# Attention scores in runs of two slot blocks and two heads, packed over five PSUM banks, with the context matmuls in one group

## The chip, the cores and the metric

The kernel runs on one core of a Trainium2 chip. The metric is the device time of one execution in microseconds. Names used for the engines: PE is TensorE (its matmuls; PEld its weight loads), ACT is ScalarE, DVE is VectorE, POOL is GpSimd and SP is SyncE, whose queue issues most transfers. L701 means line 701 of the kernel before.

## The reference

Sixteen batches of a residual self-attention with a mask. Each batch has 1024 tokens of 512 features, and 8 heads of 64 features. Queries, keys and values are the same projection `q`.

```python
def _L0_cond_ref(x, mask, Wq, Wo):          # x: (16, 512, 1024), mask: (16, 1024) of 0 and 1
    xt = jnp.transpose(x, (0, 2, 1))
    q = xt @ Wq.T
    qh = q.reshape(B, T, NH, dk).transpose(0, 2, 1, 3)
    scores = scale * jnp.einsum('bhqd,bhkd->bhqk', qh, qh)
    cmask = mask[:, None, None, :]
    rmask = mask[:, None, :, None]
    logits = (scores * cmask + (1.0 - cmask) * NEG) * rmask
    attn = jax.nn.softmax(logits, axis=-1)
    ctx = jnp.einsum('bhqk,bhkd->bhqd', attn, qh)
    ctx = ctx.transpose(0, 2, 1, 3).reshape(B, T, D)
    out = ctx @ Wo.T
    return jnp.transpose(out, (0, 2, 1))
x = x + _L0_cond_ref(x, cond_2048, L0_cond_Wq, L0_cond_Wo)
```

## The kernel before

**What it works on.** About half of the tokens of a batch are active (mask 1). The kernel sorts the active tokens of each batch into "slots", gathers their rows with indirect transfers, and does the attention over the slots only; the tokens with mask 0 all get one mean row. The width A of a batch is the number of slots that are computed: 544 for batches 0 to 4, 528 for batches 5 to 13, 512 for the last two. A slot block is 128 slots, so a batch has four whole blocks and, where A is over 512, a tail of 32 or 16 slots.

**Precision.** `query` (L513) projects with pairs of fp16 numbers, and the result q is again split into a high half h and a low half l, both fp16 (`qsplit`, L529 to L531). Four transfers on SP (L540 and on) lay them out per pair of heads in a tile `xx` of 128 partitions and four planes. For the first head of the pair, plane 0 holds h on partitions 0 to 63 and l on 64 to 127, and plane 1 holds l and h. Planes 2 and 3 hold the same for the second head.

**Scores** (`scores`, L701). For a head and a block, four matmuls: two column halves of A/2, and for each half two matmuls over all 128 partitions. Plane [h; l] against plane [h; l] gives h.h + l.l; against plane [l; h] it gives h.l + l.h. They write a tile `pss` of two PSUM banks, and the pool `ps_s` has two such tiles. ACT takes the exponential of the tile (L705), with the sum of each row as a second output (the row "ACTIVATION_READ_ACCUMULATOR"), into a tile `p` (12 buffers, which the tail's exponentials share).

**Tail scores** (L676) are those of the 32 tail slots of four heads at once: sixteen matmuls with 32 weight columns each, into a `pss` tile. ACT (L680) takes their exponential, DVE splits it, and four SP transfers (L692, L693) bring it to a tile `pt`.

**Context** (`attend`). For a pair of heads, 16 fp32 products (32 matmul records) with 64 weight columns each (L726) accumulate attention times values, head 0 into partitions 0 to 63 and head 1 into 64 to 127 of a tile `pav` of two banks (pool `ps_av`). The tail's part (L730) is added with two or four full-width matmuls, and ACT copies the result to a tile `c` (L734).

**The rest of PE's work**, called fill here: transposes of the gathered rows (`xt`, L486), the query projection (L513), values (L569), the output projection (`project`, L817) and small transposes for the softmax's shift and sums (L628, L637, L764). All of these write a pool `ps_m` of two single banks. These banks are emptied by ACT (q at L516, v at L572, the high half of x at L444) or DVE (the residual sum at L822, the low half of x at L445). So the eight banks are 4 for scores, 2 for context and 2 for all the rest.

**Order.** The loop in `run` goes over batches b, and in each over 18 steps: for each p from 0 to 3 (a pair of heads, 2p and 2p+1) the four blocks i, and two steps for the tail scores, at places 2 and 13. A step emits the scores of head 2p, some fill, the scores of head 2p+1, and fill again. The fill is one list `m` for the batch, in which pieces have costs; it belongs to the next batch's projection (n = b+1) and the previous batch's output (o = b-1). `share` says how much of it each step gets. The context group of a pair is emitted at the second step (i = 1) of the next pair, and its tail part at the third. Each step issues one indirect transfer on POOL from a list (`issue`). A scheduler orders each engine's instructions by their places in the program and by when they are ready in its own model; `behind` pins an instruction behind another on its engine, and `high_priority(offset=HPO)` moves one forward. The order on each engine is then fixed.

## Time and profile before

| what | value |
|---|---|
| median of 3 runs | 1041.18 us (1039.56 to 1042.92) |
| the profiled execution | 1033.88 us |
| its span, first to last instruction | 1032.2 us |
| mean granted TensorE clock | 0.995 |
| PE busy in 480 to 512 us | 31.49 of 32.00 us |
| ACT busy in 480 to 512 us | 22.42 of 32.00 us |
| DVE busy in 480 to 512 us | 22.17 of 32.00 us |
| first and last start of L701 | 33.1 and 1007.8 us |

A group line of the profile has the line, the engine, the operation and its tiles (written <- read), the shape and the count; then the busy time in us and the mean length in ns of one; then the idle time of the engine just before these instructions and what ended it. A busy time counts overlapping instructions once. The length of a matmul includes its way through the array, and the next one starts long before it ends, so the distance between starts tells what one costs. A shape such as 128*64 says that the weights have 128 rows and 64 columns. A line of the waits has who waited for whom: us in total, times, the longest.

### The profile page before, as it was taken

The numbers are of one execution on the slowest core, as the hardware profiler recorded it, in microseconds if no ns is written. First come the engines' busy times: TensorE is split into PE (matmuls) and PEld (weight loads), VectorE is DVE, ScalarE is ACT, GpSimd is POOL, SyncE is SP. The second block draws the span as 40 slices with busy tenths as digits, with TensorE's granted clock in tenths as the row PEclk, the third lists the DMA queues.
The fourth block names the chain that finished last, engine by engine and source line by source line (L and its number), as shares of the span: only waits on it lengthen the run. The fifth ranks groups of instructions, "written<-read, shape, count | busy, mean of one in ns | idle before, by whom it ended". The sixth has DMA issues, their size and how long they took to land. (4 is left out here: it accounts for less than half of the span.)

```text
span 1032.2 us, 23511 instructions
## 1 busy us (share of the span) xinstructions
PE 988.2 (96%) x8455; PEld 685.0 (66%) x8455; DVE 725.1 (70%) x2410; ACT 659.5 (64%) x1702; POOL 300.8 (29%) x307
## 2 busy tenths in 40 slices
PE   7798999999999999999999999999999999999996
PEld 6576667666676766767666676767666666776563
DVE  6897668676775767877666787767777777666653
ACT  5876767557667666667667567756667667665550
POOL 3101013223311232233232333323232322325562
PEclk9999999999999999999999999999999999999999
DMA  6746546557554586575657565576565666556652
GB/s 199 231 139 183 136 134 161 183 161 206 165 142 128 150 239 172 151 209 148 190 157 227 172 169 168 163 203 185 163 210 138 192 184 184 151 142 191 185 183 95
DMA packets 78795, 177.73 MB, mean 172 GB/s; under 512 B 14688, under 2 KB 20576, under 8 KB 78672
## 3 DMA queue, kind: packets, MB, share of 16 engines
q1 hardware_dynamic: 57584, 108.40, 38.8%
q0 software_dynamic: 21088, 67.75, 20.9%
q8 instruction: 69, 1.13, 0.5%
q14 instruction: 54, 0.44, 0.1%
HBM read 91.49 MB, written 33.91 MB: 121 GB/s over the span
## 5 line engine op out<-in xcount | busy, mean ns | idle before, releaser
L705 ACT ACTIVATE p<-pss,nm 128x528 f32<-128x528 f32 (+2 forms) x512 | 359.5, 706 | 169.6 <-PE pss L701 160.0
L701 PE MATMUL pss<-xx 128*128 128x264 f16 (+2 forms) x2048 | 300.9, 276 | 6.1 <-ACT p L705 5.2
L726 PE MATMUL pav<-p,v 128*64 128x264 f32 (+2 forms) x2048 | 243.3, 390 | 0.0
L701 PEld LDWEIGHTS <-xx 128*128 128x128 f16 x2048 | 194.2, 99 | 62.4 <-issue 25.1
L726 PEld LDWEIGHTS pav<-p,v 128*64 128x64 f32 x2048 | 141.4, 137 | 85.7 <-issue 13.5
L901 POOL DMA_INDIRECT y_out<-xa,idx x68 | 73.5, 1081 | 285.4 <-PE pss L701 101.6
L513 PE MATMUL pm<-xh,wqh 128*128 128x264 f16 (+5 forms) x512 | 142.2, 278 | 4.1 <-DVE xa L822 3.4
L513 PE MATMUL pm<-xl,wqh 128*128 128x264 f16 (+5 forms) x512 | 141.6, 277 | 0.2 <-DVE xl L445 0.2
L513 PE MATMUL pm<-xh,wql 128*128 128x264 f16 (+5 forms) x512 | 141.7, 277 | 0.0
L395 POOL DMA_INDIRECT xa<-x_in,idx x68 | 68.6, 1009 | 201.7 <-PE pss L701 81.1
L513 PEld LDWEIGHTS <-wqh 128*128 128x128 f16 x1024 | 98.3, 99 | 24.0 <-issue 7.5
L705 ACT ACTIVATION_READ_ACCUMULATOR p<-pss,nm 128x1 f32 x512 | 103.9, 203 | 0.0
L901 POOL DMA_INDIRECT y_out<-xi,idx x60 | 72.6, 1211 | 97.0 <-PE pss L701 26.5
L817 PE MATMUL pm<-woh,ch 128*128 128x512 f16 x240 | 91.1, 379 | 0.0
L817 PE MATMUL pm<-woh,cl 128*128 128x512 f16 x240 | 90.9, 379 | 0.0
L817 PE MATMUL pm<-wol,ch 128*128 128x512 f16 x240 | 90.9, 379 | 0.0
L395 POOL DMA_INDIRECT xi<-x_in,idx x60 | 61.3, 1021 | 95.3 <-PE pss L701 31.9
L516 ACT ACTIVATE q<-pm 128x264 f32<-128x264 f32 (+5 forms) x128 | 50.2, 392 | 59.9 <-PE pm L513 59.3
L822 DVE SCALAR_TENSOR_TENSOR xa<-pm,xa 128x512 f32<-128x512 f32 x60 | 41.3, 689 | 56.4 <-PE pm L817 52.7
L817 PEld LDWEIGHTS <-ch 128*128 128x128 f16 x480 | 46.1, 98 | 44.8 <-issue 0.9
L799 DVE TENSOR_TENSOR c<-c,rb 128x528 f32<-128x528 f32 (+2 forms) x64 | 45.4, 710 | 43.0 <-DMA rb<-rd 21.3
L888 DVE TENSOR_TENSOR xi<-xi,ub 128x512 f32<-128x512 f32 (+1 forms) x60 | 40.8, 688 | 41.8 <-PE pss L701 41.2
(223 smaller groups left out, 1509.6 us busy)
## 6 DMA issues: line engine op xcount, KB each, us to landing
xx<-hl SPq DMA_DIRECT2D x224, 136.0 KB
xm<-x_nat_in SPq DMA_DIRECT2D x56, 512.0 KB
rb<-rd SPq DMA_DIRECT2D x72, 132.0 KB
rb<-rd SPq DMA_DIRECT2D x40, 136.0 KB
pt<-c SPq DMA_DIRECT2D x36, 132.0 KB
pt<-p SPq DMA_DIRECT2D x36, 132.0 KB
ub<-ud SPq DMA_DIRECT2D x16, 256.0 KB
xx<-hl SPq DMA_DIRECT2D x32, 128.0 KB
```

The lines of the kernel that those rows point to most:

```text
L395: dma = self.nc.gpsimd.indirect_dma_start(out=tile[:n], out_offset=None, in_=self.x, in_offset=bass.IndirectOffsetOnAxis(ap=idx, axis=0))
L513: self.beat = nc.tensor.matmul(pq, lhsT=w[:, c, e * P:(e + 1) * P], rhs=xx[:, c, cols], start=(k == 0), stop=(k == 3 * DC - 1)).ins
L516: nc.scalar.activation(s["q"][:, e, cols], pq, AF.Copy, scale=1.0 / (SX * SW))
L701: self.beat = nc.tensor.matmul(pt[:, g, :CH], lhsT=xx[:, 2 * k, i * P:(i + 1) * P], rhs=xx[:, 2 * k + a, g * CH:(g + 1) * CH], start=(a == ...
L705: self.exp = [nc.scalar.activation(t.rearrange("p (g c) -> p g c", g=2), pt[:, :, :CH], AF.Exp, bias=s["nm"][p // HG][:, p % HG:p % HG + 1 ...
L726: mm = nc.tensor.matmul(s["pav"][k * DK:(k + 1) * DK, g, :CH], lhsT=s["v"][p][:, i, k * DK:(k + 1) * DK], rhs=ps[k][:, cols], start=(i == ...
L799: self.once(nc.vector.tensor_tensor(c[:, :A], c[:, :A], s["rb"][p], ALU.mult), self.beat if p < 3 else None)
L817: nc.tensor.matmul(po[:cols.stop - cols.start], lhsT=a[:, e, cols], rhs=w[:, e, :], start=(e == 0 and k == 0), stop=(e == DC - 1 and k == 2))
L822: self.nc.vector.scalar_tensor_tensor(x, po, 1.0 / (SX * SW), x, ALU.mult, ALU.add)
L888: self.once(self.nc.vector.tensor_tensor(x[:n], x[:n], s["ub"][:n], ALU.add), self.beat)
L901: dma = self.nc.gpsimd.indirect_dma_start(out=self.out, out_offset=bass.IndirectOffsetOnAxis(ap=idx, axis=0), in_=x, in_offset=None)
```

## The change

**Scores.** `scores(b, p, u)` now does a pair of heads p and two slot blocks (2u and 2u+1) in one run of 16 matmuls, so there are eight runs a batch, at the steps i = 0 and i = 2. The four results ("places": head 0 and 1, block 0 and 1 of each) lie one behind the other, A columns each, in the first five banks of one tile of six banks, from column `FIRST[A]` on. A matmul can't cross a bank, so each place is cut where a bank ends. The cross terms h.l + l.h are done as before on 128 partitions. The product h.h is done with 64 partitions of weights: plane 0's partitions 0 to 63 for the first head, plane 3's partitions 64 to 127 for the second. The two heads' pieces are issued in turn and never share a bank; the one piece that would (the second place's end, from column 1024 on) stays on 128 partitions. The product l.l is left out, except in that piece. All matmuls of a run are pinned behind one another. The first waits for all exponentials of the run before (`left`), which ACT does in the order of places 3, 0, 1, 2.

**Context.** `attend` does a pair's whole context at once, right behind the first run of the next pair, in banks 4 and 5 of the same tile from column 240 on: first the half in bank 5, then the half in bank 4 (which the fourth place reaches too, so it waits for that exponential), then the tail's part and the copy. The next run's matmuls in bank 4 wait for the copy.

**Around it.** The tail scores use banks 0 and 1 of the tile and move to places 3 and 12 of the steps. The fill's shares change to almost nothing behind the first run and most of it behind the second. The copies of q and v on ACT get `high_priority`. The first step of each pair issues two indirect transfers on POOL. Some pieces of fill change places, and a piece of cost 1.0 that does nothing is put in.

```diff
+FIRST = {544: 40, 528: 54, 512: 0}
...
-        self.ps_s = pool("ps_s", 2, space=PS)
-        self.ps_av = pool("ps_av", 1, space=PS)
         self.ps_m = pool("ps_m", 2, space=PS)
+        self.begun = ExitStack()
+        self.ps_0 = self.begun.enter_context(tc.tile_pool(name="ps_0", bufs=2, space=PS))
+        self.ps_w = self.begun.enter_context(tc.tile_pool(name="ps_w", bufs=1, space=PS))
+        self.context_out, self.left = None, []
+        self.main = lambda: pool("ps_s", 1, space=PS).tile([P, 6, 512], F32, tag="s", name="pss")
...
+    def needs(self, i, *others):
+        for o in others:
+            self.tc.add_manual_dep(i, o.name, mybir.DependencyInfo(mybir.DependencyClass.Sync, mybir.DependencyReason.DATA),
+                                   reason="the same banks")
+
+    def other_banks(self, i, *others):
+        for o in others:
+            self.tc.declare_no_dep(i, o, reason="other banks")
...
-        nc.scalar.activation(s["q"][:, e, cols], pq, AF.Copy, scale=1.0 / (SX * SW))
+        with self.tc.high_priority(offset=HPO):
+            nc.scalar.activation(s["q"][:, e, cols], pq, AF.Copy, scale=1.0 / (SX * SW))
...
-        nc.scalar.copy(v, pv)
+        with self.tc.high_priority(offset=HPO):
+            nc.scalar.copy(v, pv)
...
-            pt = self.ps_s.tile([P, 2, 512], F32, tag="s", name="pss")
+            pt = self.ps[:, 0:2]
...
+    def scores(self, b, p, u):
...
+        xx = s["xx"][p]
+        flat = self.ps.rearrange("p k n -> p (k n)")
+        first = FIRST[A]
+        places = [(k, 2 * u + i, first + (2 * k + i) * A) for k in range(2) for i in range(2)]
+        last = []
+        out = self.context_out
+
+        calls, lanes = [], ([], [])
+        for j, (k, i, at) in enumerate(places):
+            rows = slice(i * P, (i + 1) * P)
+            h = xx[k * DK:(k + 1) * DK, 3 * k, :]
+            cuts = [at] + [c for c in (512 * (j + 1),) if at < c < at + A] + [at + A]
+            for c0, c1 in zip(cuts, cuts[1:]):
+                cols = slice(c0 - at, c1 - at)
+                calls.append((c0, c1, xx[:, 2 * k, rows], xx[:, 2 * k + 1, cols]))
+                if j == 1 and c0 == 1024:
+                    calls.append((c0, c1, xx[:, 2 * k, rows], xx[:, 2 * k, cols]))
+                else:
+                    lanes[k].append((c0, c1, h[:, rows], h[:, cols]))
+        for j in range(max(map(len, lanes))):
+            calls += [l[j] for l in lanes if j < len(l)]
+        banks = [c[0] // 512 for c in calls]
+        for n, (c0, c1, w, x) in enumerate(calls):
+            with self.behind(*last), self.tc.high_priority(offset=HPO if n else 0):
+                m = nc.tensor.matmul(flat[:, c0:c1], lhsT=w, rhs=x, start=banks[n] not in banks[:n], stop=banks[n] not in banks[n + 1:])
+            if out and banks[n] < 4:
+                self.other_banks(m.ins, out)
+            elif out and banks[n] not in banks[:n]:
+                self.needs(m.ins, out)
+            if n == 0 and self.left:
+                self.needs(m.ins, *self.left)
+            last = [m.ins]
...
+        for j in (3, 0, 1, 2):
+            k, i, at = places[j]
+            t = self.sb([P, C], F32, "p", 12)[:, :A]
+            e = nc.scalar.activation(t, flat[:, at:at + A], AF.Exp, bias=s["nm"][p // 2][:, p % 2 * 2 + k:p % 2 * 2 + k + 1],
+                                     scale=SCALE, accum_out=s["z"][:, 2 * p + k, i:i + 1]).ins
...
+    def attend(self, b, p, after=None):
...
+        pav = self.ps[:, 4:6, 240:240 + CH]
+        first = []
+        exps = self.left if after else []
+        for g in (1, 0):
+            cols = slice(g * CH, (g + 1) * CH)
+            for i in range(3, -1, -1):
+                for k in (1, 0):
+                    with self.behind(*(first or ([after] if after else []))), self.tc.high_priority(offset=HPO):
+                        mm = nc.tensor.matmul(pav[k * DK:(k + 1) * DK, g], lhsT=s["v"][p][:, i, k * DK:(k + 1) * DK],
+                                              rhs=ps[k, i][:, cols], start=(i == 3), stop=(i == 0 and A == 512))
+                    self.other_banks(mm.ins, *exps[1 - g:])
+                    if g == 0 and i == 3:
+                        self.needs(mm.ins, *exps[:1])
+                    first = first or [mm.ins]
...
-        S.insert(2, (0, None))
-        S.insert(13, (1, None))
+        S.insert(3, (0, None))
+        S.insert(12, (1, None))
...
-                share = [(1.2, 0) if i is None else ((1.0, 0.6), (0.1, 0.5), (0.9, 1.0), (0.9, 0.9))[i] for _, i in S]
+                share = [(0, 0) if i is None else ((0, 0.3), (0.4, 0.4), (1.3, 1.3), (1.2, 1.2))[i] for _, i in S]
...
-                            self.scores(b, p, None)
-                    else:
-                        ps = [self.scores(b, 2 * p, i)]
-                        if i == 2 and whole:
-                            whole.pop()()
+                            self.tail_scores(b, p)
+                    elif i % 2 == 0:
+                        self.scores(b, p, i // 2)
                     fill(share[st][0], st == N - 1)
-                    if i is not None:
-                        ps.append(self.scores(b, 2 * p + 1, i))
...
+                    if i == 0:
+                        for f in todo:
+                            f(self.beat)
+                        todo = []
+
+                    for _ in range(1 + (i == 0) if b < B - 2 else -(-len(self.urgent + self.spare) // (N - st))):
                         self.issue()
...
-                            free.setdefault(st + 3 + (p == 2), []).append(L(self.recip_rows, b, p))
+                            free.setdefault(st + 3, []).append(L(self.recip_rows, b, p))
```

## The prediction

> **What bounds the kernel now.** I read the busy times first, then the costliest groups, then PE's order of time in the middle of the span, then the waits, then ACT's order of time. From the page:
>
> ```profile
> PE 988.2 (96%) x8455; PEld 685.0 (66%) x8455; DVE 725.1 (70%) x2410; ACT 659.5 (64%) x1702; POOL 300.8 (29%) x307
> L705 ACT ACTIVATE p<-pss,nm 128x528 f32<-128x528 f32 (+2 forms) x512 | 359.5, 706 | 169.6 <-PE pss L701 160.0
> L701 PE MATMUL pss<-xx 128*128 128x264 f16 (+2 forms) x2048 | 300.9, 276 | 6.1 <-ACT p L705 5.2
> L726 PE MATMUL pav<-p,v 128*64 128x264 f32 (+2 forms) x2048 | 243.3, 390 | 0.0
> ```
>
> ACT idles because it waits for PE's scores (169.6 us before the exponentials); PE hardly ever waits for ACT (5.2 us). So the end is set by how densely PE streams. The mean of 276 ns is no price, since matmuls overlap; the price is the distance between starts, in the timeline of PE:
>
> ```profile
> 481.09 0.61 PE L701 MATMUL pss<-xx 128*128 128x264 f16 x4
> 481.63 0.41 PE L486 MATMUL pm<-ident,xt 16*128 16x16 f32 x4
> 481.98 0.29 PE L513 MATMUL pm<-xh,wqh 128*128 128x264 f16 x1
> ...
> 490.14 0.61 PE L701 MATMUL pss<-xx 128*128 128x264 f16 x4
> 490.59 0.17 PE L307 MATMUL pm<-eh,on 128*128 128x3 f16 x1
> 490.61 0.61 PE L701 MATMUL pss<-xx 128*128 128x264 f16 x4
> 491.15 3.78 PE L726 MATMUL pav<-p,v 128*64 128x264 f32 x32
> 494.87 0.62 PE L701 MATMUL pss<-xx 128*128 128x264 f16 x4
> ...
> 516.48 0.38 PE L817 MATMUL pm<-wol,ch 128*128 128x512 f16 x1
> 516.70 0.38 PE L817 MATMUL pm<-woh,cl 128*128 128x512 f16 x1
> 517.01 0.63 PE L676 MATMUL pss<-xx 128*32 128x264 f16 x16
> 517.57 0.33 PE L628 MATMUL pm<-ident,smcol 128*128 128x128 f32 x1
> ```
>
> Read from it: four 264-column matmuls take 0.45 us (490.14 to 490.59), 0.1125 each; a 512-column one 0.216 (twelve starts from 514.33 to 516.70 average 0.2155). So a column costs 0.417 ns and a matmul 2.4 ns on top. From the last score to the context group 0.54 passes in place of 0.45 (490.61 to 491.15): the change of array shape costs 0.09. The same stands at L817 to L676 (517.01 less 516.70 is 0.31, not 0.216), at the way back (0.46 of matmul in 0.56, below), and into the 16-row transposes (481.63 less 481.09 is 0.54). I take **0.095 us a switch**. The sixteen 32-column-wide matmuls of L676 last 0.56 with a switch, so 0.46, 0.029 each: a quarter of 0.1125, four side by side. Narrow tiles do run together here.
>
> ACT and the waits:
>
> ```profile
> 503.95 0.70 ACT L705 ACTIVATE p<-pss,nm 128x528 f32<-128x528 f32 x1 [1.00 <-PE pss L701]
> 504.64 0.69 ACT L705 ACTIVATE p<-pss,nm 128x528 f32<-128x528 f32 x1
> 505.32 1.05 ACT L425 ACTIVATE xm<-xm 128x1024 f32<-128x1024 f32 x1
> 506.27 0.19 ACT L425 ACTIVATION_READ_ACCUMULATOR xm<-xm 128x1 f32 x1
> ```
> ```profile
> PE pss L701 <- ACT p L705: 5.2, 11, 0.6
> PE pav L730 <- DMA pt<-p: 6.0, 7, 1.8
> ```
>
> An exponential takes 0.69 us of ACT from start to start, its sum included. The eleven waits of a score matmul for ACT are 0.47 us each.
>
> **The change, part by part.**
>
> 1. *Fewer columns.* A run does one pair of heads and two blocks of 128 slots. Before, that is 16 matmuls of half the width A: 16 x 0.1125 = 1.80 us for A=528. After: the cross terms on all 128 rows, 4 x 528 columns in 8 pieces (cut at bank ends): 2112 x 0.417 + 8 x 2.4 = 0.900. One 86-column piece of h.h stays on 128 rows: 0.038. The other seven are on 64 rows: pieces of 458, 70, 442 columns in the lower half, 426, 102, 410, 118 in the upper, issued in turn. In order and side by side, the upper half ends last: 0.193 (first piece below), then 102 and 410 columns above start behind it, then 118: 0.463. Sum 1.401, saving 0.399. For A=544 the same working gives 1.853 - (0.927 + 0.046 + 0.489) = 0.391, for A=512 1.747 - (0.864 + 0.432) = 0.451. Five batches are 544 wide, nine 528, two 512, with 8 runs each: 15.6 + 28.7 + 7.2 = **-51.6 us**. No 64-row pair is in the trace. Bounds: if the halves do not overlap, the seven pieces cost 0.862, not 0.463, and 0.399 of saving is 0; perfect balance (2026 columns halved, 0.43) would give 4 us more. The 32-wide quads are the nearest row, so I take overlap. The small pieces have a second bound: the 16-row transposes take (0.35 - 0.095)/4 = 0.064 each where a 16-column matmul should need 0.01; if 64-row matmuls have that floor, three pieces per run lose about 0.02 each, 8 us in all.
>
> The Trainium skill, "TensorE: Matmul & The Clock Gate" (Part 3, "Measured speedup vs the span model"), lists 3.07x for four row tiles, so about 77% of the ideal; the L676 row has 97% for column tiles. By the page the two lanes would take 0.60 in place of 0.463, 18 us less gain.
>
> 2. *More switches.* Before, each pair of heads has two: into the context group and out. After: 128 rows to 64 rows, then to the 64-wide context group directly, then back; and in the second run two more. Three more for 64 pairs: 192 x 0.095 = **+18.2 us**.
>
> 3. *One score buffer in place of two.* The scores fill up to five banks, held once. The first matmul of a run waits for all four exponentials of the run before; all later work queued on PE stands behind it. From the last matmul's start, ACT starts 0.32 later (the fourth of the matmuls that start at 508.00 begins at 508.34, ACT at 508.66), so four exponentials are done after 0.32 + 4 x 0.69 + 0.1 = 3.2 us. What hides this: a pair lasts (1007.8 - 33.1)/64 = 15.2 us; without scores 3.6, context 3.8, its tail 0.35 and tail scores 0.3 it has 7.2 us of projections, which the new shares divide 1.1 to 5.0: 1.3 us behind the first run, together with 4.2 of context, and 5.9 behind the second. First run: 5.5 against 3.2, free. Second: 5.9 against 3.2 plus ACT's other work in that stretch. That is (659.5 - 512 x 0.69)/64 = 4.8 us a pair; less the context copy 0.6 and one half-batch sum 1.25 it is 2.95, and 5.0/6.1 of it is 2.4. So 0.3 us of slack: closed, but narrowly. The tail scores are worse: they move one step later (third place to fourth) and sit in banks 0 and 1 behind only 2.6/6.1 of 7.2 = 3.1 us. They come 0.1 us late at best, and by 1.4 if ACT did one sum first. I take the 0.45 of the waits now seen, for 28 tail groups: **+12.6 us**. Bounds of the whole part: nothing (PE order fills the holes with other projections) to 64 x 1.05 (a sum of 1.25 in front, less some slack) plus 28 x 1.0, 95 us. I am near the low end because the nearest row, L701's present wait, is rare.
>
> 4. *Context in one group behind the run.* The same 32 matmuls. Its first half uses bank 5, which no score holds; the second half needs bank 4, so the exponential of the fourth block, done 1.0 us after the run, against 1.8 us of first half: free, unless a sum of 1.25 us is ahead on ACT (then 0.4). The tail transfer pt is issued one step later and needed at the group's end, some 7 us later; landing now ends 7 waits of 6.0 us in all: from -6 to +6, taken 0. The copy of the context must be done before the next run reaches bank 4, 0.9 us into it; 1.3 us of projections and this hide its 0.6.
>
> 5. *At nothing:* copies of q (0.39) and v (0.6) go ahead of exponentials on ACT, which is the 2.4 above; two transfers instead of one are issued on POOL per first step, whose 29% hides it; the reciprocal of the third pair comes one step earlier, with three transfers on SP, whose queue gets pt's four a step later. Twelve p buffers hold eight of a pair, four of the next run and, for a while, a tail. If the tail's transfers land late, the fourth exponential waits; 3 us of margin cover this.
>
> Sum: -51.6 + 18.2 + 12.6 = -20.8. The profiled execution lasts 1033.88 (span 1032.2), so 1013.1. It is 0.7% under the median of 1041.18; the forecast for the median is 1041.2 - 20.8 = **1020.4 us**.
>
> **Rivals.**
>
> - *ACT takes the place of PE in the second half of each pair.* Four exponentials come at once where before one came every 1.9 us, so the evacuations that PE's two other buffers need stand in the same queue. It decides from (51.6 - 18.2 - 12.6)/64 = 0.33 us of stall in each second run, on top. At 0.8 (between 0.33 and 1.05 and nearer the top, as each pair has a sum) it costs 51 us: 1041.2 - 20.8 + 51 = 1071. For it: 0.3 us of slack. Against: ACT is at 64%, and sums may run during the 1.4 us of a score run, when it has no exponential. 0.19.
> - *The stalls are spread and eat the gain:* PE's other buffers are freed late by 0.08 us on the mean over 252 evacuations by ACT (128 q, 64 v, 60 xh), 20 us: 1041. Scores in small pieces no longer fill in between. 0.09.
> - *The halves don't overlap*, or both wait for one another at bank ends: no saving, 1041.2 + 18.2 + 12.6 = 1072. Against: the quads of L676. 0.06.
> - *Weights of a half can't be loaded under its own matmul.* The 16-row transposes at 0.064 hint at it. A load of 0.098 (L701's own row) exposed for 3.5 matmuls a run is 0.34, 44 us: 1064. Against: 32-wide quads at full rate with the same loads. 0.05. The Trainium skill's page just named has it, in "The mechanism": loads overlap matmuls only where the row group differs. L701 on full rows contradicts it, with loads hidden at 0.1125 spacing.
>
> **How the numbers follow.** The forecast has 0.61; its own range is 1003 (no stall at all: 1008, and some now seen waits gone) to 1036. What this measurement can tell from no change is about 0.3%, 3 us. Faster: 0.61 and a little of the second rival, 0.62. Within 0.3%: 0.08. Slower: 0.19 + 0.06 + 0.05, 0.30. The range 1002 to 1068 leaves out the no-overlap case, the upper half of ACT's and a little of the forecast: 0.19.
>
> **What would show it.** Right: h.h matmuls of the two halves starting in pairs; score runs of about 1.4 us plus a switch; PE's waits for p summing to 10 to 20 us, at the tail scores; context still 3.6. Wrong: waits of the first score matmul for p in most runs (ACT), or starts of 64-row matmuls one behind the other. It fails most easily on the second half's 0.3 us.

## The result, and the profile after

The changed kernel takes **1107.8 us** (median of four, 1102.99 to 1115.91) against 1041.65 us (1039.56 to 1042.92): 1.0645 times the time, with a 95% interval of 1.0579 to 1.0711. It is 66 us slower; the forecast was 1020.4, 21 us faster. The profiled execution took 1108.16 us, with a span of 1106.3 us (74.1 more than before) and a mean granted clock of 0.948 (0.995 before). The kernel before was profiled in an execution of 1033.88 us, below its median, which is why the spans differ by more than the medians.

The page of the changed kernel first: the busy times, the slices of granted clock, and the groups that answer to those of the prediction (L740 scores, L754 exponential, L774 context).

```profile
PE 1000.5 (90%) x8327; PEld 611.4 (55%) x8327; DVE 745.1 (67%) x2410; ACT 658.9 (60%) x1702; POOL 300.5 (27%) x307
PEclk8898899999999999899999999999899989999698
L754 ACT ACTIVATE p<-pss,nm 128x528 f32<-128x528 f32 (+2 forms) x512 | 355.4, 703 | 169.5 <-PE pss L740 131.5
L774 PE MATMUL pss<-p,v 128*64 128x264 f32 (+2 forms) x2048 | 245.4, 392 | 3.4 <-ACT p L754 3.4
L740 PE MATMUL pss<-xx 128*128 128x86 f16 (+31 forms) x1920 | 220.3, 287 | 11.1 <-issue 5.2
```

The scores' busy time fell from 300.9 to 220.3 us, and PE as a whole is busier than before: 1000.5 for 988.2. More busy time for less work means that something else on PE takes longer per instruction; a PEclk digit under 9 says where to look. PE is idle for 106 us of the span, where it was 44.

One stretch of steady state, at the head of batch 7, shows all of it in the timeline of PE (columns: start, length, engine, line, what it writes and reads, count, and in brackets the idle time before it with what ended that).

```profile
501.31 0.40 PE L582 MATMUL pm<-two,xx 128*128 128x64 f16 x8
501.54 1.67 PE L740 MATMUL pss<-xx 128*128 128x458 f16 x16
503.14 3.78 PE L774 MATMUL pss<-p,v 128*64 128x264 f32 x32
506.86 0.44 PE L608 MATMUL pm<-ident,qt 128*128 128x128 f32 x2
507.05 0.49 PE L782 MATMUL pss<-pt,vt 128*128 128x264 f32 x2
507.38 0.60 PE L498 MATMUL pm<-ident,xa 128*128 128x128 f32 x4
508.92 0.66 PE L498 MATMUL pm<-ident,xa 128*128 128x128 f32 x4 [0.94 <-DVE tmp L611]
509.41 1.67 PE L740 MATMUL pss<-xx 128*128 128x458 f16 x16
511.01 0.66 PE L498 MATMUL pm<-ident,xa 128*128 128x128 f32 x4
513.40 0.63 PE L498 MATMUL pm<-ident,xa 128*128 128x128 f32 x4 [1.73 <-DMA xa<-x_in,idx]
514.93 0.47 PE L582 MATMUL pm<-two,xx 128*128 128x64 f16 x8 [0.91 <-DVE xl L457]
515.53 0.33 PE L816 MATMUL pm<-ident,rcol 128*128 128x128 f32 x1
516.23 0.41 PE L498 MATMUL pm<-ident,xt 16*128 16x16 f32 x4 [0.37 <-DVE rr L819]
...
517.08 0.43 PE L525 MATMUL pm<-xh,wqh 128*128 128x264 f16 x1
517.30 0.43 PE L525 MATMUL pm<-xl,wqh 128*128 128x264 f16 x1
```

Three things are to be seen. A score run lasts 1.60 us from start to start (501.54 to 503.14, 509.41 to 511.01), and the context is still one group with the length it had. Then, at the head of the batch, PE waits four times between 507.98 and 516.23, 3.95 us in all: each time for a buffer of the pool `ps_m`, or for the rows that are to go through one. And behind these waits, from 516.86 on, a projection matmul takes 0.22 us from start to start where 0.1125 is its price. A table by stretch of the same place shows why (columns: stretch, length, busy time of each engine with its instructions, granted clock, share of the DMA engines, GB/s):

```profile
509.00:513.00 4.00, 2.67 (x24) 1.63 (x24) 2.10 (x4) 2.10 (x6) 2.35 (x3) 1.00 0.92 258
513.00:516.50 3.50, 1.69 (x17) 1.17 (x17) 1.57 (x3) 3.50 (x9) 0.97 (x1) 1.00 0.34 97
517.00:520.00 3.00, 3.00 (x27) 1.69 (x25) 3.00 (x9) 2.02 (x5) 0.00 (x0) 0.50 0.09 23
520.00:523.00 3.00, 3.00 (x36) 2.04 (x29) 1.79 (x7) 1.19 (x3) 0.92 (x1) 0.97 0.92 287
```

PE is busy for 58% of 7.5 us, the granted clock then drops to 0.50, for some 3.4 us, and comes back. So these waits are paid twice: once as idle time, and again as half speed behind them. The heads of the other batches are alike, though not the same: in each of the batches 1 to 13 PE waits between 7 and 16 us from the batch's first score matmul, 0.2 to 2.7 us at a time and 3.1 us in all on the mean, and the clock drops at 12 to 15 us. The wait for gathered rows stands in six of them.

The largest waits of PE in the whole trace (columns: who waits for whom; us in total, times, longest), and below them what is listed for `xl` in the kernel before:

```profile
PE pm L582 <- DVE xl L457: 11.9, 10, 2.2
PE pm L498 <- DMA xa<-x_in,idx: 9.5, 6, 2.7
PE pm L328 <- ACT q L529: 7.6, 9, 0.9
```

```profile
PE pm L594 <- DVE xl L445: 0.2, 1, 0.2
PE pm L513 <- DVE xl L445: 0.2, 1, 0.2
PE pm L764 <- DVE xl L445: 0.2, 1, 0.2
```

The head of batch 7 in the kernel before has eight transposes in one go, twice, with scores or the context between, and no wait:

```profile
471.60 1.06 PE L701 MATMUL pss<-xx 128*128 128x264 f16 x8
472.50 1.04 PE L486 MATMUL pm<-ident,xa 128*128 128x128 f32 x8
473.38 0.61 PE L701 MATMUL pss<-xx 128*128 128x264 f16 x4
473.92 3.78 PE L726 MATMUL pav<-p,v 128*64 128x264 f32 x32
477.63 1.09 PE L486 MATMUL pm<-ident,xa 128*128 128x128 f32 x8
478.56 1.06 PE L701 MATMUL pss<-xx 128*128 128x264 f16 x8
```

**The account.** Three sums over the records of PE in both traces: *idle* is the sum of all gaps over 40 ns; *half clock* is the time in which the granted clock was 0.5; *lost* is what the matmuls started in that time took beyond their price at full clock (columns x 0.417 ns + 2.4). Idle went from 36.2 to 98.9 us (+62.7), half clock from 12.2 us in 3 stretches to 117.3 us in 20, lost from 3.5 to 48.4 (+44.9). The two steps on scores save 51.6 - 18.2 = 33.4 us. So 62.7 + 44.9 - 33.4 = 74.2 us, and the span grew by 74.1. That the two agree so closely is partly luck: the 33.4 is the forecast's own figure, and another count of *lost* (half of the time at half clock in which PE isn't idle) gives +42.4 in place of +44.9.

In the 13 batches from 1 to 13, where the pattern repeats, a batch has 4.3 us of idle time (1.2 before) and 5.0 us at half clock (0 before) and lasts 3.6 us longer. (A batch is counted from its first score matmul to that of the next.) The rest is at the ends: batch 0 +7.4, batch 14 -6.4, batch 15 +25. Some 10 us of the last are a stop at 1033 to 1043 us, in which a score run stands still with nothing shown that it waits for, ACT and DVE do next to nothing either, and from 1035.6 on the clock is at half for 17.1 us. Of the other profiles only that of s1_after512 has such a stop, in the same score run. It stays unexplained, and whether the executions that were not profiled had it isn't known.

### The profile page after: what moved, and what is told of

The parts are those of the page before. It is cut to its first block, busy times and chain, and to the rows that moved or that the text cites. A ratio compares the mean times of both kernels' runs of the same rounds, so it can differ in the third digit from the quotient of the medians.

```text
span 1106.3 us, 23204 instructions
## 1 busy us (share of the span) xinstructions
PE 1000.5 (90%) x8327; PEld 611.4 (55%) x8327; DVE 745.1 (67%) x2410; ACT 658.9 (60%) x1702; POOL 300.5 (27%) x307
## 3 DMA queue, kind: packets, MB, share of 16 engines
q8 instruction: 68, 1.11, 0.4%
## 4 chain that ended last, share of the span: by engine, by line
PE 75%; ACT 8%; DVE 8%; DMA 4%; issue 3%; another core or an unknown queue 1%; POOL 1%; SPq 1%; POOLq 0%; DVEq 0%; ACTq 0%
PE pss L774 18%; PE pm L525 15%; PE pss L740 15%; PE pm L869 15%; ACT p L754 5%; PE pm L498 2%; PE pss L782 2%; PE pss L687 2%; DVE xl L457 2%; DMA xa<-x_in,idx 1%; PE pm L816 1%; PE pss L869 1%; PE warm L366 1%; DMA pt<-p 1%
## 5 line engine op out<-in xcount | busy, mean ns | idle before, releaser
L754 ACT ACTIVATE p<-pss,nm 128x528 f32<-128x528 f32 (+2 forms) x512 | 355.4, 703 | 169.5 <-PE pss L740 131.5
L774 PE MATMUL pss<-p,v 128*64 128x264 f32 (+2 forms) x2048 | 245.4, 392 | 3.4 <-ACT p L754 3.4
L740 PE MATMUL pss<-xx 128*128 128x86 f16 (+31 forms) x1920 | 220.3, 287 | 11.1 <-issue 5.2
L774 PEld LDWEIGHTS pss<-p,v 128*64 128x64 f32 x2048 | 142.0, 138 | 92.7 <-issue 17.5
L953 POOL DMA_INDIRECT y_out<-xa,idx x68 | 72.8, 1071 | 414.9 <-DVE xa L874 116.8
L740 PEld LDWEIGHTS <-xx 128*128 128x128 f16 (+1 forms) x1920 | 109.0, 97 | 95.0 <-issue 38.6
L525 PE MATMUL pm<-xh,wqh 128*128 128x264 f16 (+5 forms) x512 | 151.6, 296 | 3.8 <-DVE rr L819 1.2
L525 PE MATMUL pm<-xl,wqh 128*128 128x264 f16 (+5 forms) x512 | 151.2, 295 | 0.0
L525 PE MATMUL pm<-xh,wql 128*128 128x264 f16 (+5 forms) x512 | 151.0, 295 | 0.0
L407 POOL DMA_INDIRECT xa<-x_in,idx x68 | 77.1, 1134 | 115.6 <-ACT xm L437 49.1
L754 ACT ACTIVATION_READ_ACCUMULATOR p<-pss,nm 128x1 f32 x512 | 104.5, 204 | 0.0
L786 ACT COPY c<-pss 128x528 f32<-128x528 f32 (+2 forms) x64 | 38.4, 599 | 82.2 <-PE pss L782 43.1
L457 DVE SCALAR_TENSOR_TENSOR xl<-pm,xh 128x512 f16<-128x512 f32 (+2 forms) x73 | 42.8, 608 | 44.5 <-ACT xh L456 27.2
L874 DVE SCALAR_TENSOR_TENSOR xa<-pm,xa 128x512 f32<-128x512 f32 x60 | 41.2, 687 | 45.4 <-PE pm L869 37.3
```

The source lines that it names most:

```text
L407: dma = self.nc.gpsimd.indirect_dma_start(out=tile[:n], out_offset=None, in_=self.x, in_offset=bass.IndirectOffsetOnAxis(ap=idx, axis=0))
L457: self.xs = nc.vector.scalar_tensor_tensor(self.xl[dst], src, SX, self.xh[dst], ALU.mult, ALU.subtract).ins
L525: self.beat = nc.tensor.matmul(pq, lhsT=w[:, c, e * P:(e + 1) * P], rhs=xx[:, c, cols], start=(k == 0), stop=(k == 3 * DC - 1)).ins
L740: m = nc.tensor.matmul(flat[:, c0:c1], lhsT=w, rhs=x, start=banks[n] not in banks[:n], stop=banks[n] not in banks[n + 1:])
L754: e = nc.scalar.activation(t, flat[:, at:at + A], AF.Exp, bias=s["nm"][p // 2][:, p % 2 * 2 + k:p % 2 * 2 + k + 1], scale=SCALE, accum_out ...
L774: mm = nc.tensor.matmul(pav[k * DK:(k + 1) * DK, g], lhsT=s["v"][p][:, i, k * DK:(k + 1) * DK], rhs=ps[k, i][:, cols], start=(i == 3), sto ...
```

## The experiments

All ratios are to the kernel before on the same chip, and the intervals are 95%. Idle, half clock and lost are the sums just defined, and the last two columns are lengths of batches, all in us and from the profiled execution of each kernel. The executions were not all on one chip (the kernel before takes 1033.8 us on the one of e1 to e5 and some 1042 on the others), so the same batch of 65 us can differ by some 0.5 us between them; the ratios are free of this.

| kernel | ratio, interval | idle | half clock | lost | batches 1 to 13, mean | batch 15 |
|---|---|---|---|---|---|---|
| before | 1 | 36.2 | 12.2 | 3.5 | 62.1 | 71.4 |
| after | 1.0645 (1.0579 to 1.0711) | 98.9 | 117.3 | 48.4 | 65.7 | 96.2 |
| e1_busy | 1.0776 (1.0734 to 1.0819) | 84.8 | 54.6 | 17.5 | 66.7 | 86.3 |
| e2_fullrows | 1.0668 (1.0616 to 1.0720) | 81.1 | 64.4 | 27.3 | 66.6 | 80.2 |
| e3_order | 1.0393 (1.0355 to 1.0432) | 81.1 | 75.4 | 30.9 | 64.6 | 76.8 |
| e5_defer | 1.0817 (1.0775 to 1.0859) | 114.7 | 50.3 | 21.9 | 66.8 | 80.7 |
| e6_banks | 1.0457 (1.0403 to 1.0511) | 101.3 | 57.9 | 23.9 | 65.5 | 74.8 |
| e7_share | 1.0645 (1.0585 to 1.0705) | 100.1 | 89.1 | 37.3 | 66.7 | 74.6 |
| s0_before512 | 0.9243 (0.9210 to 0.9277) | 34.7 | 24.8 | 9.1 | 56.6 | 78.1 |
| s1_after512 | 1.0706 (1.0667 to 1.0746) | 175.2 | 170.5 | 64.3 | 65.9 | 99.0 |
| s2_three512 | 0.9105 (0.9059 to 0.9151) | 62.0 | 43.0 | 17.6 | 56.2 | 75.2 |
| s3_three512_order | 0.9058 (0.9008 to 0.9108) | 57.9 | 38.6 | 17.5 | 56.2 | 76.3 |
| f2_hold_order | 1.0238 (1.0203 to 1.0272) | 77.5 | 47.8 | 20.5 | 63.8 | 74.6 |
| f0_before_hold | 1.0016 (0.9993 to 1.0038) | 45.2 | 18.8 | 6.4 | 62.5 | 76.0 |

**Is the clock low because PE waits, or because of the 64-row matmuls?** e1_busy adds work that no one needs to the changed kernel: 15 matmuls of 512 columns a batch into bank 5, five each behind the third and the fourth transpose and behind the last values.

```diff
+    def idle(self, n):
+        w = self.w["q"][0]
+        with self.behind(self.pe):
+            for _ in range(n):
+                self.nc.tensor.matmul(self.ps[:, 5, :], lhsT=w[:, 0, :P], rhs=w[:, 1, :], start=True, stop=True)
...
+            if b > 1 and k in (2, 3):
+                self.idle(IDLE)
```

> The changed kernel with 15 more matmuls of 512 columns per batch (from batch 2 on), whose results nobody uses: five each behind the third and fourth transposes and behind the values at the head of a batch, where PE was seen to wait 3 to 5 us per batch. Theory (the head of a batch has only small matmuls between two buffers, PE idles, and the idling halves the granted clock): the added 14 x 15 x 0.216 = 45 us of work fall into the idle time, time at half clock falls from 117 us to under 60, and the time falls by 15 to 35 us, to some 1075 to 1093. Rival A (the clock is lowered by the 64-row matmuls, which use half of the array): time at half clock stays near 117 us and the time rises by 10 to 45. Rival B (the waits alone cost the time, the clock is a side effect without price): half clock falls, time stays within 5 us.

It came out at 1.0776 and missed the number: it is 1.3 points, some 14 us, slower than the changed kernel, and not faster. What it says is in batches 1 to 13. A batch lasts 1.0 us longer for 3.2 us of added work (1.5, if the chips' 0.5 is counted in), so some 2 us of it were paid for: idle time fell from 4.3 to 3.7 us a batch, and half clock from 5.0 to 1.3 us, with every 64-row matmul still in place. So it is the waits that bring the clock down and not the shape of the matmuls. And the clock has a price of its own, against rival B, since 0.6 us less idle time can't pay for 2. But to keep PE busy with waste doesn't pay here: it bought back half to two thirds of what it cost.

**Does the score saving reach the end at all?** e2_fullrows takes the 64-row tiles out: h.h on 128 rows everywhere, which also computes l.l again.

```diff
-                if j == 1 and c0 == 1024:
-                    calls.append((c0, c1, xx[:, 2 * k, rows], xx[:, 2 * k, cols]))
-                else:
-                    lanes[k].append((c0, c1, h[:, rows], h[:, cols]))
-        for j in range(max(map(len, lanes))):
-            calls += [l[j] for l in lanes if j < len(l)]
+                calls.append((c0, c1, xx[:, 2 * k, rows], xx[:, 2 * k, cols]))
```

> The changed kernel with h.h (and with it l.l again) on all 128 rows for all pieces: 16 full matmuls a run, no 64-row tiles; everything else as changed. Theory (the 64-row part does what was computed: 0.399 us a run less work, 3 x 64 switches more): PE has 51.6 - 18.2 = 33 us more to do, of which a part falls into holes; the time rises by 15 to 33 us to 1123 to 1141, with half clock still near 117 us. Rival A (64-row matmuls or their switches lower the clock): half clock falls under 30 us and the time falls below 1090.

1.0668, which overlaps 1.0645, so the 15 to 33 us that were expected do not show in the total. But the total hides two differences. In batches 1 to 13 a batch lasts 66.6 us against 65.7: of the 2.1 us of work that are given back (33.4 over sixteen batches) 0.9 reach the time, or 1.4 if the chips' 0.5 is counted in, and the rest takes the place of waits and half clock (3.8 and 3.7 us a batch, where the changed kernel has 4.3 and 5.0 us). And batch 15 is 16.0 us shorter, since e2's profile lacks the stop at 1033 us. So in the changed kernel PE's stream sets the time only in part: the saving is real, and a third to more than a half of it went into waiting. The 3.7 us at half clock that are left in a batch without any 64-row tile speak once more against the shape as its cause.

**Does the order of the fill matter?** The change moved some pieces. e3_order puts two of the previous batch's four output projections (`P_(2)` and `P_(3)` in the list) back between what fills the common banks at a head.

```diff
-                    m += q(2, 1) + pk(n, 0) + (take if b else []) + tp(n, 0) + P_(2) + bt(n, 0) + q(3, 0)
-                    m += P_(3) + q(3, 1) + v(2) + tc(1) + [(0, L(self.means, n))] + tv(1)
+                    m += q(2, 1) + pk(n, 0) + P_(2) + (take if b else []) + tp(n, 0) + q(3, 0) + bt(n, 0)
+                    m += q(3, 1) + v(2) + tc(1) + [(0, L(self.means, n))] + P_(3) + tv(1)
```

> The changed kernel with the third and fourth output projections and the gathers of the next batch but one back at their places of before (second projection ahead of the gathers, last one between the values and the tail's values), so that 2.6 us of projection stand right at the batch's end. Theory (holes at the head of a batch for want of large work there): waits before transposes, values and small transposes fall from 54 us to 25 to 45, half clock falls to 50 to 100 us, the time by 10 to 40 us. Rival B (ACT's four exponentials at once are what holds PE up): no change beyond 5 us, since runs and shares are untouched.

1.0393: 2.5 points better, some 26 us, the best full version. In batches 1 to 13 it is 1.1 us a batch (0.6 with the chips' 0.5); part of the rest is that its profile lacks the stop in batch 15. The two largest of PE's waits that are left have one name:

```profile
PE pm L498 <- DVE xl L457: 15.9, 16, 1.1
PE pm L582 <- DVE xl L457: 13.9, 13, 1.1
```

A transpose or a value matmul wants a bank that DVE has not finished reading. Three other versions don't beat it. e5_defer keeps P_(2) ahead and sends the last projection to the next batch's head, between the transposes:

```diff
-                    m = sums + x[:2] + second + x[2:4] + (value(b, 3) if b else []) + rows + x[4:] + pk(b, 1)
+                    D_ = project(b - 2, 3) if b > 1 else []
+                    m = sums + x[:1] + D_ + x[1:2] + second + x[2:4] + (value(b, 3) if b else []) + rows + x[4:] + pk(b, 1)
```

> The changed kernel with the last output projection of a batch put off by one batch, to stand between the first and second transposes at its head, and the third projection ahead of the gathers as before the change. Theory: 2.6 us of work fill the head; waits before transposes, values and small transposes fall to under 25 us, half clock to under 40 us, the time to 1015 to 1060. Rival B (four exponentials at once): the waits only move, to the score runs or to other places, and the time stays above 1090.

1.0817, a miss: the waits for gathered rows, 9.5 us in the changed kernel, became 23.2. Why the rows come later isn't shown. A gather's buffer is also one that a projection's result is scattered from, and in the changed kernel POOL waits 8.6 us for such scatters before its gathers; but in e5_defer's trace it waits for none. e6_banks has e3's order, all transposes between the first context and the second run, and the first two of them in banks 0 and 1 of the scores; e7_share is the same with all transposes in the common banks.

```diff
+            elif b > 1 and k < 2:
+                pt = self.ps[:, k, :].rearrange("p (c n) -> p c n", c=DC)
...
-                    m = sums + x[:2] + second + x[2:4] + (value(b, 3) if b else []) + rows + x[4:] + pk(b, 1)
+                    if b:
+                        m = sums + x[:4] + second + x[4:] + value(b, 3) + rows + pk(b, 1)
...
+                if 0 < b < B - 1:
+                    share[:2] = [(0, 0.9), (0.4, 0.4)]
```

> The changed kernel with the projections and gathers in the order of before (as in e3_order), and with the transposes at a batch's head all between the first context group and the second score run, the first two of them into score banks 0 and 1, which are free there, the others into the two common banks. Theory (the head waits because four transposes pass through two banks, each of which is held until ACT and then DVE have read it, behind exponentials): the four transposes run without a wait, PE's waits before transposes fall from 24 us under 8, all waits between the span's ends from 65 to under 45, half clock falls under 50 us, and the time is 0.97 to 1.01 of the kernel before. Rival B (ACT's four exponentials a run set the pace): the exponentials and their order are as before, so the time stays above 1.03 of the kernel before.

> As e6_banks, with the same pieces of work in the same places of the list and the same shares, but all transposes in the two common banks as in the changed kernel. Theory: with only two banks the transposes wait for one another and for the exponentials; time 1.03 to 1.07 of the kernel before, waits before transposes over 15 us, half clock over 50 us. If it is as fast as e6_banks, the order did it and not the banks.

1.0457 with the score banks, 1.0645 without: two more banks at the head alone are worth 1.9 points in the same order, 1.2 us a batch. The wait of the transposes for DVE's xl, 29.2 us in e7_share, is 9.5 in e6_banks. But e6_banks missed its 0.97 to 1.01: other waits (the tail's transfer, 11.2) rose in its place, it is no gain over e3_order, and it stays above 1.03, as its rival said. So the banks at the head are a part of the cause and not the whole.

**One more common bank.** With every batch 512 wide, two blocks of two heads fill exactly four banks and the context one, so a third bank for `ps_m` is free. s0 and s1 are the kernels before and after with all batches 512 wide (the tail slots and their part of the result are left out). s2 is s1 with the context in one bank and three common banks; s3 adds the order of e3.

```diff
-        self.ps_m = pool("ps_m", 2, space=PS)
+        self.ps_m = pool("ps_m", 3, space=PS)
...
-        self.main = lambda: pool("ps_s", 1, space=PS).tile([P, 6, 512], F32, tag="s", name="pss")
+        self.main = lambda: pool("ps_s", 1, space=PS).tile([P, 5, 512], F32, tag="s", name="pss")
...
-        pav = self.ps[:, 4:6, 240:240 + CH]
+        pav = self.ps[:, 4, :].rearrange("p (g c) -> p g c", g=2)
...
```

> The kernel before with all batches 512 slots wide: tail scores, tail values and the tail's context are left out, so slots from 512 on keep the mean row. It is the yardstick for the next three. Both theories: 0.93 to 0.97 of the kernel before.

> The changed kernel with the same leaving out (all batches 512 wide, no tails), two common banks as in the change. Theory (PE waits for the two common banks, and the clock follows): 1.03 to 1.08 of s0_before512, waits before transposes and values over 25 us, half clock over 60 us. If it is under 1.01 of s0, the tails or the cuts at bank ends are what costs.

> As s1_after512, and with three common banks in place of two: at 512 wide the context of a pair fits into one bank, so the score tile takes five. Nothing else differs. Theory (two common banks with scores in lumps are too few): waits before transposes, values and small transposes fall to less than half of s1's, half clock under 40 us, the time to 0.95 to 1.01 of s0_before512. Rival B (four exponentials at once and one score buffer): within 1% of s1_after512.

> As s2_three512, with the projections and gathers in the order of before (e3_order's edit). Theory: with three banks the order matters less than the 2.4% that it was worth with two: within 1.5% of s2, and at 0.95 to 1.00 of s0_before512, where the 64-row saving of 16 x 8 x 0.451 = 58 us less 18 us of switches shows as at least half.

At this width the change as it stands costs even more, 1.0706 / 0.9243 = 1.158, far above the 1.08 expected at most. One more bank takes 1116.9 us to 951.1, by 166 us: 9.7 us in each of the batches 1 to 13, and 23.8 in batch 15, where s1 has its stop. Then the change is a gain: 0.9105 / 0.9243 = 0.985 of its own before, 0.980 with the order. That is 13 and 17 us of the 40 (58 less 18) that the expectation of s3 counts, so less than half. No run gives the kernel before a third common bank, which it would have room for at this width too; so how much of the gain is the change's own is not shown. The largest waits of PE in s1, and then in s2:

```profile
PE pm L498 <- DMA xa<-x_in,idx: 43.6, 11, 7.4
PE pm L642 <- DVE smcol L633: 19.5, 7, 10.4
PE pss L740 <- ACT p L754: 15.9, 14, 5.2
```

```profile
PE pss L740 <- ACT p L754: 12.2, 9, 4.8
PE pm L498 <- DMA xa<-x_in,idx: 8.8, 6, 2.4
PE pm L498 <- DVE xl L457: 7.0, 4, 3.3
```

Of the 19.5 us for `smcol` 10.4 are one wait, behind the stop. Not only the waits for xl go (12.8 and 6.2 at L498 and L582 in s1): the waits for gathered rows fall from 43.6 to 8.8. That late banks delay the gathers by way of the projections and their scatters is an idea that the traces don't show: POOL's gathers wait 3.8 us for such scatters in s1 and 4.9 in s2. What tops the list in s2 is the wait that the prediction was about, that of a run for its exponentials. At 528 and 544 the scores and the context need 2640 and 2720 columns, more than the 2560 of five banks, so this can't be done at full width as it is.

**How long a bank is held.** The last pair tests the same cause on the full width. DVE computes the low half of the gathered x from the high half in SBUF, so that a bank is free after ACT's copy, one DVE instruction (0.68 us) earlier. The same edit goes into e3_order and into the kernel before. It leaves out the low half of x; the number of instructions and the length of DVE's (median 682 and 684 ns) stay.

```diff
-                self.xs = nc.vector.scalar_tensor_tensor(self.xl[dst], src, SX, self.xh[dst], ALU.mult, ALU.subtract).ins
+                self.xs = nc.vector.scalar_tensor_tensor(self.xl[dst], self.xh[dst], 1.0, self.xh[dst], ALU.mult, ALU.subtract).ins
```

> The changed kernel in the order of e3_order, and DVE computes the low half of the gathered x from the high half in SBUF instead of from the transposes' PSUM bank, so the bank is free after ACT's copy alone, some 0.6 to 0.7 us earlier. This leaves out the low half of x (it becomes zero); the number of instructions on every engine stays. Theory (two common banks, held too long at a batch's head): e3_order showed PE waiting 33.0 us for DVE's xl in all and lost 30.9 us to the half clock; most of the 33 and about half of the clock loss go: 25 to 45 us under e3_order (1.0393), so 0.996 to 1.015 of the kernel before; half clock under 50 us. Rival (the banks wait for ACT's copies behind the exponentials in its queue, and DVE was only the last link): PE's waits move to ACT's xh or to the next buffer, ratio 1.030 to 1.040, half clock still about 75 us.

> The kernel before with the same edit (low half of x computed from the high half in SBUF, the bank free after ACT's copy; leaves out the low half of x). Theory: with 16 small score pieces per pair between the uses of the two common banks, an earlier release is worth nearly nothing: 0.990 to 1.002. Rival (an earlier release helps any order alike, and the run's lumps have no part in it): as large a gain here as in f2_hold_order against e3_order, 0.96 to 0.975.

The kernel before: 1.0016 (0.9993 to 1.0038), nothing, as expected; its PE waits for xl are 0.6 us in the whole trace. The changed one: 1.0238 against 1.0393, so 1.5 points or some 16 us, less than the 25 expected at least, and below the 1.030 that the rival gave as its lowest. The waits of f2_hold_order say where the rest is:

```profile
PE pm L498 <- DVE rr L819: 8.3, 12, 0.7
PE pm L582 <- ACT xh L456: 6.2, 12, 0.5
PE pm L498 <- ACT xh L456: 4.9, 14, 0.4
```

About a third of the 33 us for xl moved one link up, to ACT's copy of the same bank. Between the two profiled spans (14.4 us) 10.4 us are clock and only 3.6 idle: the waits left are shorter (0.7 us at most in these rows, 1.1 in those of e3_order).

ACT's order in the changed kernel shows what else its copies share a queue with:

```profile
512.87 0.70 ACT L754 ACTIVATE p<-pss,nm 128x528 f32<-128x528 f32 x1 [1.68 <-PE pm L498]
513.47 0.19 ACT L754 ACTIVATION_READ_ACCUMULATOR p<-pss,nm 128x1 f32 x1
513.56 1.09 ACT L456 ACTIVATE xh<-pm 128x512 f16<-128x512 f32 x2
514.55 0.69 ACT L754 ACTIVATE p<-pss,nm 128x528 f32<-128x528 f32 x1
```

The run's last matmul started at 510.87; its signal to ACT stands in the trace at 512.85, and the first exponential begins at 512.87. Why the signal came 2.0 us late the profile doesn't show, and it is rare: where ACT waits for PE, its exponential starts 0.31 us behind the last score matmul in the median. The four exponentials of a run stand in one queue with the copies that free the banks. No run here divides the rest of f2's 2.4% between this and the waits elsewhere; that stays open.

## Why the prediction was wrong, point by point

1. *Fewer columns, -51.6.* Right. A run was to last 1.401 us and two switches, 1.59; it lasts 1.60, here and in the median of the 99 runs of sixteen matmuls that had the full clock and no wait behind them. The two halves run together: in the run behind 509.41 the 458- and the 426-column piece both start at 510.46, the 442 and the 410 both at 510.70. By the Trainium skill, "TensorE: Matmul & The Clock Gate" (Part 3, "Measured speedup vs the span model"), with 77% of the ideal, it would have been 0.60 - 0.463 = 0.137 us more; the trace doesn't bear that out here, and the row was the better price. The no-overlap and weight-load rivals fall with it.
2. *More switches, +18.2.* Right, as part of the same 1.60 us.
3. *One score buffer, +12.6.* Right as a term: PE's waits for `p` are 2.9 us at L740, 3.4 at L774 and 2.8 at L687, 9.1 in all, and the second half's "0.3 us of slack" held. Wrong as the whole price of lumps. **This is the step that failed**: the sum took the waits for the score buffer as all that one buffer in place of two costs, and put the waits at the other banks at nothing. Its lower bound said that "PE order fills the holes with other projections", but all of this fill passes through two common banks. Before, eight score pieces of 0.45 us (the expectation of f0 counts them as 16) and the context stood between the uses of these banks in each pair and gave ACT and DVE time to empty them. Afterwards two lumps of 1.6 us do so, and at the head of a batch several transposes stand behind one another with a bank held for 1.3 us each (ACT's copy, then DVE's subtraction). The prediction's second rival named this ("PE's other buffers are freed late") and sized it by a mean of 0.08 us over 252 evacuations, 20 us. PE's waits for xl alone went from 0.6 us to 23.1 (11.9, 4.2, 3.7, 3.1 and 0.2 at five lines). The waits for gathered rows add 9.5 (2.5 before). The stalls aren't spread: 3.1 of the 4.3 us of idle time in a batch stand in one place, 0.2 to 2.7 us each.
4. *Context behind the run, 0.* Right, one wait of 3.4 us in the whole trace.
5. *At nothing.* The copies put ahead and the moved pieces of fill were priced as queue time on ACT alone. The order of the fill is worth up to 2.5 points (e3_order), some 0.6 to 1.1 us a batch in steady state.

What no step and no rival had is the granted clock: 44.9 us, beside the 62.7 of idle time that bring it about. The rival with the largest chance, ACT as the new bound, gave a slower kernel (1071) by another mechanism than the one found: a run was to wait for its exponentials, and those waits are the 9.1 us above.

**Shown:** that the added time is PE's waiting and the clock behind it (the account); that the clock follows the waits (e1_busy); that PE's work sets the time only in part (e2_fullrows: 0.9 to 1.4 of 2.1 us a batch); that the common banks are a cause, at 512 by a third bank, at full width by two more banks at the head (e6 and e7) and by a shorter hold that helps the new order and not the old (f2 and f0). **Open:** the last 2.4% at full width, of which ACT's queue may be a part; why the gathered rows come late; the stop in batch 15; and a version of the change that beats the kernel before on the whole task; none was found.

## What to carry to other kernels

Small pieces of one job between two uses of a shared buffer are worth something that no count of columns shows: before they are packed into one run, list what else passes through the buffers that are left, how long each is held from the write to the last read, and how much other work stands between two uses in the new order. A kernel whose PE is 96% busy has a second price on each wait, the clock behind it; here 62.7 us more of waiting came with 44.9 us more of half speed, so on the mean a wait cost about 1.7 times its length. And where a saving on the busiest engine doesn't show, give it back (as in e2_fullrows), and compare stretches of steady state and not only totals: here 0.9 to 1.4 of 2.1 us a batch came back, and one stop near the end hid it in the total.

## What the runs showed of the hardware

- Waits under 2 us, four within 8.2 us, were enough for a drop to half clock: 0.94, 1.73, 0.91 and 0.37 us, then 0.50 for 3.4 us. In the changed kernel a lone wait of 0.83 to 0.88 us (L328, nine of the batches 1 to 13) was not followed by one. In between it can go either way: in e3_order the batches 2 to 13 have two waits of 1.07 to 1.11 us each, starting some 2.4 us apart, and in five of the twelve the clock dropped. A stretch of steady state lasts 3.4 us or, where the next one follows, 6.8. The Trainium skill, "TensorE: Matmul & The Clock Gate" (Part 1, "HAM oscillation — how this bites in real kernels"), gives as the abstract rule that there should be no idle gap over about 3.4 us; this trace shows less to suffice. Its next section ("A second HAM failure mode: psum-queue depth-cycling") has this case in kind, PE idling briefly between groups as it cycles through banks, without a price; here it is 44.9 us of 1106.
- Matmuls on the lower and the upper 64 rows, with different weights and into different banks, started side by side (in 102 runs the first and the third pair 2 to 5 ns apart, the second up to 25) and cost together what the longer one costs. A change between 128 and 64 rows cost about 0.096 us, as the other changes of shape did: a 118-column piece, 0.052 us of work, starts at 510.308 and the first 64-row matmul at 510.456.
- 3.2 us of useless matmuls a batch made it 1.0 to 1.5 us longer, since they filled waits and kept the clock up (half clock 1.3 us a batch in place of 5.0).
